# Attention with top-1 experts on one core: SyncE's transfers in the program's order, the row maxima split on VectorE, one block's sums inverted in place

## The chip, the cores and the metric

The kernel runs on one core of a Trainium2 chip. The metric is device time in microseconds of one launch, the median of several executions. A profile is one further execution; its own time is given beside its span below.

## The reference

The input `x` has 4 batches of 2048 tokens of 512 numbers. Each token is normalised, and `xn` goes through two branches that are added to `x`: an attention with 16 heads of 32 numbers, and a top-1 mixture of experts in which 8 experts take at most 100 tokens each, over all batches.

```python
x = L0_attn_x
xn = _layernorm(x)
x = x + _L0_attn_ref(xn, ...) + _L0_ffn_ref(xn, ...)

# attention
q, k, v = heads(xn @ w_qkv)
q, k = spectral_filter(q, mask), spectral_filter(k, mask)   # a linear map on each head's 32 numbers
attn = softmax(q @ k.T / sqrt(32))                          # 2048 x 2048 for each head
out = (attn @ v) @ w_out + b_out

# experts
probs = softmax(hs @ w_gate); best = argmax(probs)
location = cumsum(one_hot(best)) - 1                        # kept where location < 100
out = gate * (dispatched @ w_expert + b_expert)             # zero for the others
```

## The kernel before

**Groups, blocks, windows.** The 16 heads are worked four at a time, so there are 16 groups `k` (4 batches x 4 head groups; `k % 4` is the head group, and every fourth group ends a batch). A group has four blocks `n` of 512 queries. A block walks over 16 tiles `j` of 128 keys, two tiles to a window: 8 windows to a block, 32 to a group (`GW`), 512 in all. Here window w of a group is counted from that group's start; windows 24 to 31 belong to its block 3.

**One tile `j`.** For two pairs of heads `u`, TensorE first writes minus the row maxima into two banks of the array of 8 PSUM banks (`shift`, with `negm` as operand), then the scores of a later block, whose maxima are being taken (`max_matmuls`, two more banks), then this block's own scores on top of the shift (`scores`). ScalarE takes the exponentials into the tiles `even` and `odd`; VectorE reduces the later block's scores to maxima (`max_reduce`, tile `part`). Then come the products with `v` of the tile before (`products`, one bank), which VectorE adds to `num`. The banks are handed out in rotation by `bank()` and `turns`.

**The row maxima** run 40 steps of the stream ahead of the exponentials, so that a block's maxima are complete in window 5 of the block before it. `max_negate` (L469) makes `neg`; `max_close` (L474) runs in the next window: TensorE transposes `neg` into a bank (`pn`), ScalarE copies it to `rest`, GpSimd splits it into three bf16 parts that add up to it (`row`: three casts, two subtractions), and three DMAs of 4 KB spread them into `negm`, which the first `shift` of the next block reads.

**The sum of the exponentials** is built in the tile `even` by GpSimd (`add_to`, two adds to a window) and by an accumulating DMA from `odd` (`pair`, 1 MB to a window, GpSimd's queue).

**A block's end** (`close_steps`, L627) is spread over the windows of the next block, counted from its first: window 2 `fold` (row sums by TensorE, copied to `den`, written to DRAM), 3 `fetch` (read back as 128x16, `few`), 4 `invert` (a reciprocal on VectorE, written to DRAM), 5 `spread` (four broadcast reads to `factor`), 7 `divide` (`ot` on GpSimd), 8 and 9 the output projection into `y`, 10 an accumulating DMA of `y` to the output. The very last block uses `close_last`.

**The stage of the next batch.** In a group with `k % 4 == 2` the tokens of the next batch are loaded in four chunks of 1 MB (tag `xs`, two buffers), measured by VectorE (`measure`), given the output bias by GpSimd and written to the output (`first_sums`). At that group's end the first two chunks are loaded again, and in the next group they are normalised by ScalarE and transposed.

**What sets the order.** TensorE, VectorE, ScalarE and GpSimd are called through `InOrder` (L71): their instructions stay in the order in which the program makes them. Steps are entered in an agenda, a list for every window (`at`, L747); the first half of a window's list runs after its even tile, the rest after its odd one. SyncE's DMAs are made by plain `nc.sync` calls: the planner of the language may bring them forward, wherever it reckons that they can run. SyncE works through its own queue in order, and an entry that waits for data or for a buffer holds up those behind it. All wrapped instructions carry line L82 in the profile, SyncE's DMAs their own.

Of the kernel before, what the change touches and what calls it, by code (L numbers as in the profile page):

```python
# [12 lines left out]
F32 = mybir.dt.float32  # L13
# [88 lines left out]
def attention_and_top1_experts(ctx: ExitStack, tc: tile.TileContext, a: dict, out: bass.AP):  # L102
# [14 lines left out]
    def bank():  # L117

        return array[:, next(turns), :]
# [69 lines left out]


    on = SimpleNamespace(tensor=nc.tensor, vector=nc.vector, scalar=nc.scalar, gpsimd=nc.gpsimd)
    def filter_weights(c):
        for s in range(2):
            pt, pw = bank(), bank()
            for r in range(NR):
                on.tensor.transpose(
                    pt[:, r * P : (r + 1) * P], raw[s, r // 2][:, r % 2, c * P : (c + 1) * P], ident
                )
            if s == 0:
                both = probs(c == 1)  # L200
            wt = both[:, s]
            on.scalar.copy(wt[:, 0, :], pt)
            for r in range(NR):
                at = slice(r * P, (r + 1) * P)
                on.tensor.matmul(pw[:, at], lhsT=wt[:, 0, at], rhs=filt, start=True, stop=True)
            on.scalar.copy(wt[:, 1, :], pw)
            nc.sync.dma_start(out=wd[c][:, :, s, :], in_=wt[:, 1, :].rearrange("p (r n) -> p r n", r=NR))

    xnT = seq.tile([P, NR, S], F32, name="xnT")

# [1 line left out]
    def token_stage(b):  # L212
# [5 lines left out]

        def load(n, name="xs"):
            held[n] = chunk(name)  # L220
            nc.sync.dma_start(out=held[n], in_=x[b, n])

        def measure(i):
            on.vector.bn_stats(stats[:, i, :], held[i // TQ][:, i % TQ, :])
# [5 lines left out]

        def first_sums(n):

            nc.sync.dma_start(out=o[b, n], in_=held[n])

        def scale(first=0, last=NT):
            at = slice(first, last)
# [142 lines left out]

    def load_qkv_weights(k):  # L380
        wg[k] = weights.tile([P, NR, 3, P], F32, name="wg", bufs=1)
        nc.sync.dma_start(out=wg[k], in_=wd[k % NG])

    def load_out_weights(k):
        c = k % NG
        wo[k] = weights.tile([P, DM], F32, name="wo")
        nc.sync.dma_start(out=wo[k], in_=a["L0_attn_w_out"][c * P : (c + 1) * P, :])

    def columns(out, lhsT, rhs, **flags):

# [82 lines left out]

    def max_close(k, n):  # L474

        pn = bank()[0 : HG * TQ, 0:P]
        on.tensor.matmul(pn, lhsT=negs.pop((k, n)), rhs=ident, start=True, stop=True)
        rest = small.tile([HG * TQ, P], F32, name="rest")
        row = small.tile([HG * TQ, 3, P], BF16, name="row", bufs=2)
        on.scalar.copy(rest, pn)  # L480
        on.gpsimd.tensor_copy(row[:, 0, :], rest)
        for i in (1, 2):
            on.gpsimd.tensor_tensor(rest, rest, row[:, i - 1, :], ALU.subtract)
            on.gpsimd.tensor_copy(row[:, i, :], rest)
        negms[k, n] = qkv.tile([P, QB], BF16, tag="negm", name="negm", bufs=3)
        for i in range(3):
            nc.sync.dma_start(out=negms[k, n][i::DH, :], in_=row[:, i, :])


    taken = {}  # L490
# [1 line left out]
    def expert_steps():  # L492


        def begin():
            w_exp = chunk("w_exp")
            nc.sync.dma_start(out=w_exp, in_=a["L0_ffn_w_expert"].rearrange("(r p) n -> p r n", p=P))
            b_exp = work.tile([P, DM], F32, tag="b_exp", name="b_exp", bufs=1)
            nc.sync.dma_start(out=b_exp, in_=a["L0_ffn_b_expert"].partition_broadcast(P))
            entries = small.tile([P, NTAB, ST, 2], F32, name="entries")  # L500
            for i, table in enumerate(tables):
                nc.sync.dma_start(out=entries[:, i], in_=table.rearrange("(t p) c -> p t c", p=P))
# [12 lines left out]
            bound = {"bounds_check": B * S - 1, "oob_is_err": False}  # L515
            taken.update(mv=mv, w_exp=w_exp, b_exp=b_exp, entry=entry, index=index, bound=bound, xg=xg)
# [110 lines left out]
    def close_steps(k, n, num, acc):  # L627

        b = k // NG
        held = {}  # L630

        def fold():
            den = work.tile([P, QB], F32, tag="den", name="den", bufs=1)
            on.scalar.copy(den, row_sums([acc]))
            held["sums"] = scratch.tile([HG, QB], F32, name="sums")
            nc.sync.dma_start(out=held["sums"], in_=den[0::DH, :])


        def fetch():
            held["few"] = small.tile([P, HG * QB // P], F32, name="few", bufs=2)  # L640
            nc.sync.dma_start(out=held["few"], in_=held["sums"].rearrange("h (c e) -> (h c) e", e=HG * QB // P))

        def invert():
            on.vector.reciprocal(held["few"], held["few"])
            held["inverse"] = scratch.tile([HG, QB], F32, name="inverse")
            nc.sync.dma_start(
                out=held["inverse"].rearrange("h (c e) -> (h c) e", e=HG * QB // P), in_=held["few"]
            )

        def spread():  # L650
            held["factor"] = work.tile([P, QB], F32, tag="factor", name="factor", bufs=1)
            for h in range(HG):
                nc.sync.dma_start(
                    out=held["factor"][DH * h : DH * (h + 1)], in_=held["inverse"][h].partition_broadcast(DH)
                )

        def divide():
            held["ot"] = work.tile([P, QB], F32, tag="ot", name="ot", bufs=1)
            on.gpsimd.tensor_tensor(held["ot"], num, held["factor"], ALU.mult)

        def result(t):
            if t == 0:
                held["y"] = chunk("y")
            on.scalar.copy(held["y"][:, t, :], project(k, held["ot"], t))

        def add():
            on.gpsimd.dma_start(out=o[b, n], in_=held["y"], accum_op=ALU.add)

        steps = [(2, fold), (3, fetch), (4, invert), (5, spread), (7, divide)]
        return steps + [(8, result, 0), (8, result, 1), (9, result, 2), (9, result, 3), (10, add)]  # L670

    def close_last(k, n, num, tiles, y):
# [9 lines left out]
        for t in range(TQ):  # L682
            on.vector.tensor_tensor(y[:, t, :], y[:, t, :], project(k, ot, t), ALU.add)
            if t % 2 == 1:
                nc.sync.dma_start(out=o[b, n, :, t - 1 : t + 1, :], in_=y[:, t - 1 : t + 1, :])


    load, measure, scale, normalize, turn, first_route, first_bias, first_sums = token_stage(0)
# [22 lines left out]
    nc.gpsimd.memset(nobody, 0.0)  # L711
    nc.gpsimd.memset(nobody[:, :, 0], float(FAR))
    for table in tables:
        nc.sync.dma_start(out=table.rearrange("(t p) c -> p t c", p=P), in_=nobody)

    load_out_weights(0)
    first_projections = projections(0)
    for step in first_projections[:2]:
        step()
    ahead, first_projections = first_projections[2:7], first_projections[7:]  # L720
    on.tensor, on.vector, on.scalar, on.gpsimd = (
        InOrder(tc, engine) for engine in (nc.tensor, nc.vector, nc.scalar, nc.gpsimd)
    )
    closing = {}
    for i, item in enumerate(stream[:MAX_AHEAD]):
# [21 lines left out]
    def at(window, step, *args):  # L747
        agenda[window].append(lambda: step(*args))
# [30 lines left out]
    def plan(k):  # L779
# [16 lines left out]
            return  # L796
        at(start + GW // 2, load_out_weights, k + 1)
        if k + 2 < B * NG:
            at(start + GW - 1, load_qkv_weights, k + 2)
        if k == 0:  # L800
            at(len(first_projections), load_qkv_weights, 1)
        first, last = len(first_projections) + 2 if k == 0 else 0, GW - 1
        if c == NG - 2 and b + 1 < B:

            at(start + 10, begin_stage, b + 1)
            for n in range(NQ):
                at(start + 11 + 4 * n, in_stage, 0, n)
                at(start + 18 + 4 * n, in_stage, 7, n)
            for i in range(NT):
                at(start + 13 + i, in_stage, 1, i)  # L810
                at(start + 14 + i, in_stage, 6, i)
            at(start + GW - 2, in_stage, 2)
            at(start + GW - 2, in_stage, 0, 0)
            at(start + GW - 1, in_stage, 0, 1)
        elif c == NG - 1:

            for n in (2, 3):
# [23 lines left out]
    for k in range(B * NG):  # L841
        plan(k)
        for n in range(NQ):
            num = work.tile([P, QB], F32, tag="num", name="num")
            tiles = {}
            for w in range(NW):
# [7 lines left out]
                for j in (even, odd):  # L854
# [14 lines left out]
                    while full_blocks:  # L869
                        block = full_blocks.pop(0)  # L870
                        max_negate(*block)
                        at(window + 1, max_close, *block)
                    if left:
                        products(*left)
                    left = k, n, j, tiles[j], num
# [6 lines left out]
                        adds[window + 2] = tiles[even], tiles[even - WIN]  # L882
                if last and w == NW - 2:
                    y = chunk("xs")
                    nc.sync.dma_start(out=y, in_=o[B - 1, n])
# [44 lines left out]
```

## Time and profile before

| | |
|---|---|
| median of 3 runs | 4603.65 us (4592.69 to 4610.5) |
| the profiled execution, its own time | 4607.95 us |
| its span | 4606.1 us |
| TensorE, matmuls | 4435.0 us busy, 96% of the span |
| VectorE | 3102.1 us, 67% |
| GpSimd | 3001.0 us, 65% |
| ScalarE | 2596.2 us, 56% |
| DMAs issued by GpSimd (queue q0) | 606.88 MB, 66.6% of 16 engines |
| DMAs issued by SyncE (queue q1) | 91.56 MB, 6.4% of 16 engines |

PE is TensorE, PEld its weight loads, DVE VectorE, ACT ScalarE, POOL GpSimd, SP SyncE. Matmuls overlap, and the ends of busy times are modelled, so a busy TensorE is not one at its peak. The granted clock is TensorE's, as a share of full speed. An idle time in brackets behind an instruction names what ended it.

### The profile page before, as it was taken

The page shows a single profiled execution, that of the slowest core. Times are in us where ns is not written, and L with a number is a line of the kernel's source. Part 1 is how long each engine was busy: PE and PEld are TensorE (multiplying, and loading weights), DVE is VectorE, ACT ScalarE, POOL GpSimd, SP SyncE. Part 2 cuts the span into 40 slices and gives each one's busy share as a digit, 9 for nine tenths or more (in the row PEclk, how much of TensorE's full clock was granted, in tenths as well). Part 3 has the DMA queues.
Part 4 walks back from the last instruction along what each step waited for, and adds up shares of the span by engine and source line. Part 5 has one row for each costly group of instructions (what it writes and reads, how often), then busy time and mean ns, then how long its engine had stood idle before and what let it go on. Part 6 is the DMA issues. An engine that isn't in the chain of part 4 may idle for free.

```text
span 4606.1 us, 106228 instructions
## 1 busy us (share of the span) xinstructions
PE 4435.0 (96%) x44438; PEld 1886.8 (41%) x44438; DVE 3102.1 (67%) x3625; ACT 2596.2 (56%) x4945; POOL 3001.0 (65%) x2081
## 2 busy tenths in 40 slices
PE   6999999989999999998999999999999999999986
PEld 3444443433434344443444434343343434434431
DVE  4666776765676767775567766776567676777772
ACT  3445555555555555556455555555555565555654
POOL 0467766765676666775577666767567675777766
PEclk9999999989999999999999999999999999999998
DMA  5567777886776877787577776878767776787876
GB/s 117 137 153 149 152 157 149 186 184 137 142 151 140 163 147 159 151 205 177 120 145 154 158 154 134 165 163 191 158 125 150 155 152 127 151 169 163 162 159 143
DMA packets 193234, 708.90 MB, mean 154 GB/s; under 512 B 47778, under 2 KB 54084, under 8 KB 127344
## 3 DMA queue, kind: packets, MB, share of 16 engines
q0 software_dynamic: 110576, 606.88, 66.6%
q1 hardware_dynamic: 77800, 91.56, 6.4%
q8 instruction: 348, 5.70, 0.5%
q10 hardware_dynamic: 4376, 3.67, 0.4%
q14 instruction: 134, 1.10, 0.1%
HBM read 77.09 MB, written 89.99 MB: 36 GB/s over the span
## 4 chain that ended last, share of the span: by engine, by line
PE 85%; DMA 7%; POOL 3%; issue 3%; ACT 1%; DVE 1%; SPq 0%; ACTq 0%; POOLq 0%; DVEq 0%
PE array L82 85%; DMA even<-odd 2%; POOL even L82 2%; DMA few<-sums 1%; DMA sums<-den 1%; DMA negm<-row 1%; DVE part L82 1%; ACT odd L82 1%; DMA wg<-wd 0%; POOL ot L82 0%; DMA wd<-in_L_attn_w_qkv_dram 0%; POOL table L82 0%; ACT even L82 0%; PE array L393 0%; POOL rest L82 0%
## 5 line engine op out<-in xcount | busy, mean ns | idle before, releaser
L82 DVE TENSOR_REDUCE part<-array 128x2 f32<-128x1024 f32 (+1 forms) x2312 | 2433.6, 1097 | 1271.2 <-PE array L82 1259.4
L82 POOL TENSOR_TENSOR even<-even 128x1024 f32<-128x1024 f32 x892 | 2179.2, 2568 | 218.9 <-DMA even<-odd 217.0
L82 PE MATMUL array<-k,q 32*128 32x512 f32 x8192 | 2233.1, 623 | 8.5 <-issue 4.7
L82 PE MATMUL array<-q,k 32*128 32x512 f32 x8192 | 2059.8, 596 | 1.4 <-issue 1.4
L82 ACT ACTIVATE even<-array 128x512 f32<-128x512 f32 x2048 | 1065.4, 601 | 506.0 <-PE array L82 484.6
L82 ACT ACTIVATE odd<-array 128x512 f32<-128x512 f32 x2048 | 1060.7, 602 | 451.7 <-issue 237.7
L82 POOL DMA_DIRECT2D even<-odd x511 | 463.9, 908 | 1149.1 <-ACT odd L82 929.7
L82 PEld LDWEIGHTS array<-k,q 32*128 32x128 f32 x8192 | 812.1, 184 | 196.8 <-issue 76.1
L82 PE MATMUL array<-negm,ones_b 3*128 3x512 bf16 x4096 | 800.9, 383 | 55.7 <-DMA negm<-row 29.4
L82 PEld LDWEIGHTS array<-q,k 32*128 32x128 f32 x8192 | 752.1, 186 | 13.9 <-issue 5.1
L82 DVE TENSOR_TENSOR num<-num,array 128x512 f32<-128x512 f32 x960 | 651.1, 678 | 63.0 <-PE array L82 46.5
L82 PEld LDWEIGHTS <-ones_b 3*128 3x128 bf16 x4096 | 204.0, 92 | 926.8 <-issue 781.6
L82 PE MATMUL array<-even,v 128*32 128x512 f32 x4096 | 549.5, 609 | 9.8 <-ACT odd L82 9.7
L82 PE MATMUL array<-odd,v 128*32 128x512 f32 x4096 | 550.4, 608 | 3.3 <-ACT even L82 3.1
L82 PE MATMUL array<-xnT,wg 128*32 128x512 f32 x4032 | 461.6, 592 | 2.2 <-DMA wg<-wd 1.2
L82 PE MATMUL array<-wo,ot 128*32 128x512 f32 x2048 | 258.7, 596 | 19.6 <-POOL ot L82 19.5
L82 PEld LDWEIGHTS array<-xnT,wg 128*32 128x32 f32 x4032 | 131.8, 110 | 304.5 <-issue 268.8
L82 PEld LDWEIGHTS array<-even,v 128*32 128x32 f32 x4096 | 80.9, 108 | 400.8 <-ACT odd L82 388.2
L82 PEld LDWEIGHTS array<-odd,v 128*32 128x32 f32 x4096 | 81.3, 108 | 399.2 <-ACT even L82 388.5
L82 PEld LDWEIGHTS array<-wg,xnT 128*32 128x32 f32 x8192 | 226.1, 110 | 38.1 <-issue 22.6
L82 ACT COPY y<-array 128x512 f32<-128x512 f32 x252 | 147.5, 586 | 163.4 <-PE array L82 163.2
L82 PE MATMUL array<-wg,xnT 128*32 128x128 f32 x8192 | 237.0, 273 | 0.5
(140 smaller groups left out, 1436.0 us busy)
## 6 DMA issues: line engine op xcount, KB each, us to landing
even<-odd POOLq DMA_DIRECT2D x511, 1024.0 KB
out_dram<-y POOLq DMA_DIRECT2D x63, 1024.0 KB
xs<-in_L_attn_x_dram SPq DMA_DIRECT2D x31, 1024.0 KB
out_dram<-xs SPq DMA_DIRECT2D x16, 1024.0 KB
factor<-inverse SPq DMA_DIRECT2D x252, 64.0 KB
wg<-wd SPq DMA_DIRECT2D x16, 768.0 KB
wo<-in_L_attn_w_out_dram SPq DMA_DIRECT2D x16, 256.0 KB
negm<-row SPq DMA_DIRECT2D x192, 4.0 KB
```

What stands on the lines that cost most here:

```text
L82: done = act(*args, **kwargs)
```

## The change

1. SyncE gets the `InOrder` wrapper too, from the point where the other engines have it: all its DMAs keep the program's order.
2. Some steps move in the agenda. The load of a group's projection weights (`wg`) is entered for window 30, not 31. In the stage, the loads of the four chunks stand at windows 11, 15, 20, 24 (before: 11, 15, 19, 23) and the writes `first_sums` at 19, 23, 28, 32 (before: 18, 22, 26, 30); bias and measurement of chunks 2 and 3 come one window later; the second load of chunk 0 stays at 30, that of chunk 1 moves from 31 to 33, `scale` from 30 to 31.
3. `max_close` does its split on VectorE, three casts from PSUM and two subtractions in PSUM, in four slots of the bank of `pn`. ScalarE's copy and GpSimd's five instructions go. The step is put at the head of its window's list, not at its end.
4. The last block but one, (15, 2), is closed by `fold_here`: a reciprocal on VectorE of all 128x512 sums straight out of PSUM, with no way through DRAM, and its later steps come four windows sooner: `divide` at 3, projections at 4 and 5, the accumulating DMA at 6.

```diff
     def max_close(k, n):
-        pn = bank()[0 : HG * TQ, 0:P]
-        on.tensor.matmul(pn, lhsT=negs.pop((k, n)), rhs=ident, start=True, stop=True)
-        rest = small.tile([HG * TQ, P], F32, name="rest")
+        pn = bank()[0 : HG * TQ, :].rearrange("p (i n) -> p i n", n=P)
+        on.tensor.matmul(pn[:, 0], lhsT=negs.pop((k, n)), rhs=ident, start=True, stop=True)
         row = small.tile([HG * TQ, 3, P], BF16, name="row", bufs=2)
-        on.scalar.copy(rest, pn)
-        on.gpsimd.tensor_copy(row[:, 0, :], rest)
-        for i in (1, 2):
-            on.gpsimd.tensor_tensor(rest, rest, row[:, i - 1, :], ALU.subtract)
-            on.gpsimd.tensor_copy(row[:, i, :], rest)
+        for i in range(3):
+            if i > 0:
+                on.vector.tensor_tensor(pn[:, i], pn[:, i - 1], row[:, i - 1, :], ALU.subtract)
+            on.vector.tensor_copy(row[:, i, :], pn[:, i])
         negms[k, n] = qkv.tile([P, QB], BF16, tag="negm", name="negm", bufs=3)
         for i in range(3):
-            nc.sync.dma_start(out=negms[k, n][i::DH, :], in_=row[:, i, :])
+            on.sync.dma_start(out=negms[k, n][i::DH, :], in_=row[:, i, :])
...
+        def fold_here():
+            held["factor"] = work.tile([P, QB], F32, tag="factor", name="factor", bufs=1)
+            on.vector.reciprocal(held["factor"], row_sums([acc]))
...
+        if (k, n) == (B * NG - 1, NQ - 2):
+            return [(2, fold_here), (3, divide), (4, result, 0), (4, result, 1), (5, result, 2), (5, result, 3), (6, add)]
...
-    on.tensor, on.vector, on.scalar, on.gpsimd = (
-        InOrder(tc, engine) for engine in (nc.tensor, nc.vector, nc.scalar, nc.gpsimd)
+    on.tensor, on.vector, on.scalar, on.gpsimd, on.sync = (
+        InOrder(tc, engine) for engine in (nc.tensor, nc.vector, nc.scalar, nc.gpsimd, nc.sync)
     )
...
         if k + 2 < B * NG:
-            at(start + GW - 1, load_qkv_weights, k + 2)
+            at(start + GW - 2, load_qkv_weights, k + 2)
...
             at(start + 10, begin_stage, b + 1)
-            for n in range(NQ):
-                at(start + 11 + 4 * n, in_stage, 0, n)
-                at(start + 18 + 4 * n, in_stage, 7, n)
+            for n, (come, go) in enumerate(((11, 19), (15, 23), (20, 28), (24, GW))):
+                at(start + come, in_stage, 0, n)
+                at(start + go, in_stage, 7, n)
             for i in range(NT):
-                at(start + 13 + i, in_stage, 1, i)
-                at(start + 14 + i, in_stage, 6, i)
-            at(start + GW - 2, in_stage, 2)
+                at(start + 13 + i + i // 8, in_stage, 1, i)
+                at(start + 14 + i + i // 8, in_stage, 6, i)
+            at(start + GW - 1, in_stage, 2)
             at(start + GW - 2, in_stage, 0, 0)
-            at(start + GW - 1, in_stage, 0, 1)
+            at(start + GW + 1, in_stage, 0, 1)
...
                         max_negate(*block)
-                        at(window + 1, max_close, *block)
+                        agenda[window + 1].insert(0, lambda block=block: max_close(*block))
```

All other `nc.sync.dma_start` calls become `on.sync.dma_start` (the first loads, made before the wrapper is set, stay free). One of them is the load of the output rows that the very last block adds to (L885, entered in window 510); others are the expert stage's `w_exp`, `b_exp` and `entries` (L497 to L502, entered in window 18 of group 12, with two reductions of `entries` on VectorE in the same step).

More of the change, by code (lines that the diff above doesn't have):

```diff
@@ L191, in attention_and_top1_experts @@
     on = SimpleNamespace(tensor=nc.tensor, vector=nc.vector, scalar=nc.scalar, gpsimd=nc.gpsimd)
+    on.sync = nc.sync
     def filter_weights(c):
@@ L206, in filter_weights @@
             on.scalar.copy(wt[:, 1, :], pw)
-            nc.sync.dma_start(out=wd[c][:, :, s, :], in_=wt[:, 1, :].rearrange("p (r n) -> p r n", r=NR))
+            on.sync.dma_start(out=wd[c][:, :, s, :], in_=wt[:, 1, :].rearrange("p (r n) -> p r n", r=NR))
     xnT = seq.tile([P, NR, S], F32, name="xnT")
@@ L220, in load @@
             held[n] = chunk(name)
-            nc.sync.dma_start(out=held[n], in_=x[b, n])
+            on.sync.dma_start(out=held[n], in_=x[b, n])
         def measure(i):
@@ L231, in first_sums @@
         def first_sums(n):
-            nc.sync.dma_start(out=o[b, n], in_=held[n])
+            on.sync.dma_start(out=o[b, n], in_=held[n])
         def scale(first=0, last=NT):
@@ L381, in load_qkv_weights @@
         wg[k] = weights.tile([P, NR, 3, P], F32, name="wg", bufs=1)
-        nc.sync.dma_start(out=wg[k], in_=wd[k % NG])
+        on.sync.dma_start(out=wg[k], in_=wd[k % NG])
     def load_out_weights(k):
@@ L386, in load_out_weights @@
         wo[k] = weights.tile([P, DM], F32, name="wo")
-        nc.sync.dma_start(out=wo[k], in_=a["L0_attn_w_out"][c * P : (c + 1) * P, :])
+        on.sync.dma_start(out=wo[k], in_=a["L0_attn_w_out"][c * P : (c + 1) * P, :])
     def columns(out, lhsT, rhs, **flags):
@@ L496, in begin @@
             w_exp = chunk("w_exp")
-            nc.sync.dma_start(out=w_exp, in_=a["L0_ffn_w_expert"].rearrange("(r p) n -> p r n", p=P))
+            on.sync.dma_start(out=w_exp, in_=a["L0_ffn_w_expert"].rearrange("(r p) n -> p r n", p=P))
             b_exp = work.tile([P, DM], F32, tag="b_exp", name="b_exp", bufs=1)
-            nc.sync.dma_start(out=b_exp, in_=a["L0_ffn_b_expert"].partition_broadcast(P))
+            on.sync.dma_start(out=b_exp, in_=a["L0_ffn_b_expert"].partition_broadcast(P))
             entries = small.tile([P, NTAB, ST, 2], F32, name="entries")
             for i, table in enumerate(tables):
-                nc.sync.dma_start(out=entries[:, i], in_=table.rearrange("(t p) c -> p t c", p=P))
+                on.sync.dma_start(out=entries[:, i], in_=table.rearrange("(t p) c -> p t c", p=P))
             entry = small.tile([P, ST, 2], F32, name="entry1")
@@ L635, in fold @@
             held["sums"] = scratch.tile([HG, QB], F32, name="sums")
-            nc.sync.dma_start(out=held["sums"], in_=den[0::DH, :])
+            on.sync.dma_start(out=held["sums"], in_=den[0::DH, :])
+        def fold_here():
+            held["factor"] = work.tile([P, QB], F32, tag="factor", name="factor", bufs=1)
+            on.vector.reciprocal(held["factor"], row_sums([acc]))
         def fetch():
             held["few"] = small.tile([P, HG * QB // P], F32, name="few", bufs=2)
-            nc.sync.dma_start(out=held["few"], in_=held["sums"].rearrange("h (c e) -> (h c) e", e=HG * QB // P))
+            on.sync.dma_start(out=held["few"], in_=held["sums"].rearrange("h (c e) -> (h c) e", e=HG * QB // P))
         def invert():
@@ L645, in invert @@
             held["inverse"] = scratch.tile([HG, QB], F32, name="inverse")
-            nc.sync.dma_start(
+            on.sync.dma_start(
                 out=held["inverse"].rearrange("h (c e) -> (h c) e", e=HG * QB // P), in_=held["few"]
@@ L652, in spread @@
             for h in range(HG):
-                nc.sync.dma_start(
+                on.sync.dma_start(
                     out=held["factor"][DH * h : DH * (h + 1)], in_=held["inverse"][h].partition_broadcast(DH)
@@ L684, in close_last @@
             if t % 2 == 1:
-                nc.sync.dma_start(out=o[b, n, :, t - 1 : t + 1, :], in_=y[:, t - 1 : t + 1, :])
+                on.sync.dma_start(out=o[b, n, :, t - 1 : t + 1, :], in_=y[:, t - 1 : t + 1, :])
     load, measure, scale, normalize, turn, first_route, first_bias, first_sums = token_stage(0)
@@ L713, in attention_and_top1_experts @@
     for table in tables:
-        nc.sync.dma_start(out=table.rearrange("(t p) c -> p t c", p=P), in_=nobody)
+        on.sync.dma_start(out=table.rearrange("(t p) c -> p t c", p=P), in_=nobody)
     load_out_weights(0)
@@ L884, in attention_and_top1_experts @@
                     y = chunk("xs")
-                    nc.sync.dma_start(out=y, in_=o[B - 1, n])
+                    on.sync.dma_start(out=y, in_=o[B - 1, n])
                 window += 1
```

## The prediction

> **What bounds it now.** I read the page's busy times and chain first, then TensorE's waits, then the chain and SyncE's queue around one of the waits, then the granted clock, then a quiet window.
>
> ```profile
> PE 4435.0 (96%) x44438; PEld 1886.8 (41%) x44438; DVE 3102.1 (67%) x3625; ACT 2596.2 (56%) x4945; POOL 3001.0 (65%) x2081
> PE 85%; DMA 7%; POOL 3%; issue 3%; ACT 1%; DVE 1%; SPq 0%; ACTq 0%; POOLq 0%; DVEq 0%
> PE array L82 <- DMA negm<-row: 29.4, 5, 8.8
> PE array L82 <- POOL ot L82: 19.5, 10, 7.7
> SPq L885 <- DMA out_dram<-y: 32.4, 1, 32.4
> ```
>
> TensorE sets the time; it is idle for 171 us, in few, long waits, and the last line is one entry of SyncE's queue that held it for 32 us. SyncE's queue and the chain, at the end of group 2 (the stage):
>
> ```profile
> 917.67 0.38 SPq L221 DMA_DIRECT2D xs<-in_L_attn_x_dram  x1
> 921.66 0.53 SPq L636 DMA_DIRECT2D sums<-den  x1
> 957.04 0.38 SPq L221 DMA_DIRECT2D xs<-in_L_attn_x_dram  x1
> 958.41 2.21 SPq L487 DMA_DIRECT2D negm<-row  x3
> ...
> 921.66 11.71 DMA sums<-den
> 933.39 8.54 DMA few<-sums
> 960.09 11.15 DMA negm<-row
> 942.02 0.25 DVE L82 RECIPROCAL few<-few 128x16 f32<-128x16 f32 x1 [6.64 <-DMA few<-sums]
> 943.40 0.58 PE L82 MATMUL array<-negm,ones_b 3*128 3x512 bf16 x1 [2.47 <-DVE part L82]
> 943.00:949.60 6.60, 6.20 (x31) 2.40 (x34) 4.80 (x7) 2.17 (x4) 6.60 (x5) 0.50 0.81 169
> ```
>
> Small transfers stand behind 1 MB loads that the planner brought forward (the load at 917.67 belongs to window 30 and ran in window 26): 8 KB took 11.71 us, 4 KB 11.15 us. In quiet blocks `sums` takes about 6 us. VectorE waits for `few` with its reductions behind it, TensorE for VectorE's banks; after 2.47 us of idleness the granted clock (the column before the last two) is 0.50 for 6.6 us. A window later `negm` is late, two more later the next `few`.
>
> **The gain at the stages.** TensorE's idle times there are 2.47 + 1.64 + 7.07 + 6.44 = 17.6 us after group 2, 1.60 + 8.75 + 6.53 = 16.9 after group 6, 1.60 + 6.81 + 6.01 = 14.4 after group 10. The half-clock stretches last 23.8, 20.4 and 20.4 us; the parts in which TensorE works (15.5, 10.0, 13.7) cost half of themselves, 7.7 + 5.0 + 6.9. Sum: 68.5 us. In the written order `fold` and `fetch` of blocks 2 and 3 have no 1 MB transfer just ahead of them, and `negm` goes ahead of `wg` and `xs` in window 30. What is late next: SyncE runs ahead of the windows, so chunk 0's load follows `sums` at window 11 and `first_sums` follows it at 19, both ahead of a `fetch` whose reciprocal comes some 10 us later; and chunk 0 of the second pass, behind `wg` (1.75 MB) from window 30, is normalised in 32, 13 us later. A 1 MB load moves at full pace only between the `pair` transfers (5 us of each 6.2 us window), so these are close. I take back 2 us a stage, 0 and 12 at the ends. Gain 62.
>
> **Queues that the moved steps pass.** In SyncE's queue the load of chunk 2 (window 20) waits for the write of chunk 0 to land, with block 1's `inverse` and `factor` behind it; GpSimd needs `factor` three windows later, some 20 us on, so that costs nothing unless a 1 MB transfer takes over 15 us. The second load of chunk 1 (33) waits for the write of chunk 3 (32), with block 3's `sums` behind it; `few` is due two windows later. `wg` in window 30 waits for the last projection, made by window 29: nothing. `max_close` at the head of its list puts its transpose up to half a window earlier in TensorE's queue, at the same length, and its three DMAs (0.53 us of SyncE each) ahead of that window's loads.
>
> **Group 15.** The load of L885, brought forward to group 15's first half, blocks `sums`: TensorE idles 12.54 us from 4423.8 and then runs 5.2 us at half clock: 15 us, which go, as the load now stands behind window 6 of block 2. The `negm` wait at 4510 (5.40 us) goes with GpSimd's casts, but `ot` is next in GpSimd's queue and only 2 us sooner: gain 2.
>
> **The tail.**
>
> ```profile
> 4578.21 3.47 PE L82 MATMUL array<-wo,ot 128*32 128x512 f32 x16 [7.65 <-POOL ot L82]
> 4593.17 1.32 POOL L82 DMA_DIRECT2D out_dram<-y  x1 [3.99 <-ACT y L82]
> ```
>
> Today block (15, 2) leaves its projections and its accumulating DMA (10 us, SyncE waits 10.3 us for it at the end) behind everything else. Early, its inversion costs VectorE about 3.2 us (a 128x128 reciprocal took 0.91; it grows with the columns), hidden, since no maxima are left (without that cover up to 3 us, the adds to `num` being behind it), and its DMA then stretches the last `pair` (the same neighbour stretched one to 15.80 us at 4537). The end is then the last output write, some 4 us after its issue at about 4591 to 4594, not 4604.8: gain 8, between 0 and 15.
>
> **Smaller gains.** Seven waits for `ot` at the turn of a group (1.2 to 1.9 us, 9 in all) follow GpSimd's five split instructions (3 x 0.28 + 2 x 0.42 and gaps, 2 us): gain 7. A `negm` wait behind `entries` at 3575 (1.35) and one for `wg` (1.22): 2.5.
>
> **The price of the split.** The quiet window in which a close falls:
>
> ```profile
> 1667.95 0.68 DVE L82 TENSOR_TENSOR num<-num,array 128x512 f32<-128x512 f32 x1
> 1669.08 2.42 DVE L82 TENSOR_REDUCE part<-array 128x1 f32<-128x512 f32 x3 [0.45 <-PE array L82]
> 1667.60 0.38 PE L82 MATMUL array<-square,neg 128*16 128x128 f32 x2
> 1669.00 0.59 PE L82 MATMUL array<-k,q 32*128 32x512 f32 x2
> L82 DVE COPY logits<-array 128x32 f32<-128x32 f32 x16 | 2.9, 184 | 0.0
> L82 DVE TENSOR_TENSOR chosen<-array,gate 128x128 f32<-128x128 f32 x4 | 1.2, 292 | 0.4
> ```
>
> VectorE's 67% hides that here both engines are full: a tile asks VectorE for 2 x 1.22 + 0.68 = 3.12 us and TensorE for 3.14. No cast of 16x128 from PSUM is in the trace. A copy of 32 columns takes 184 ns[...]; a subtraction 292. Each depends on the one before, which adds 35 ns (gap between `stats` and `mv`): 3 x 0.284 + 2 x 0.292 + 4 x 0.035 = 1.58 us. [...]the bank of `pn` stays shut for all of it, where ScalarE's copy freed it after 0.25.
>
> Who waits: the next eight banks are two shifts and two maxima for each `u`, and the eighth, the second maxima bank of `u` = 0, is the bank of `pn`. TensorE gets there at 1669.00, 1.0 us after the transpose's end at 1667.98. VectorE is free at 1668.63 (its add), done at 1668.63 + 1.58 = 1670.21: TensorE stalls 1.2 us, and 0.9 where VectorE is not behind (after a projection). It can't win this back, being the bound. From 0.5 (short instructions, VectorE ahead) to 1.6 (all of it), I take 1.0, between the two cases. With 63 closes whose next maxima are running: 63 us, ends 32 and 100. [...]here 1.97 us at 1456 was enough and 2.10 us at 263 was not. [...] No stall under 1.7 us stands alone before a halving here, so I count none.
>
> **Another price.** Group 12, window 18: `w_exp`, `b_exp` and `entries` are issued only after window 14's `negm`, not 100 to 400 us ahead, and VectorE's two reductions of `entries` wait with all maxima behind them. `entries` are 8-byte packets, 3584 of them; beside `pair` one set took about 7 us (3576.6 to 3584). From 3632 they have 30 us and need about that: 3 us, between 0 and 16.
>
> **Sum.** 4607.95 - 62 - 17 - 8 - 7 - 2.5 + 63 + 3 = 4577.5 us for the profiled execution; it lies 4.3 us above the median of the runs, so 4573 for a median.
>
> **Rivals.** (a) *The split is cheaper*: VectorE catches up in time, 0.5 us a close. For it: in block 2 of group 2, eight `bn_stats` pairs (0.87 us each) lengthened the block by only 2 us (67.5 against 65.6 in group 5, from first exponential to first exponential). Against it: those shut no bank. 63 becomes 32: 4542. (b) *The stage waits stay*: loads at windows 11, 19 and 30 make `few`, the measurements or ScalarE's normalising late, 8 to 10 us a stage with the half clock. For it: every one of these margins is under 5 us, and a load issued at 917.67 was still on the wire at 933. Against it: `pair` leaves gaps. 24 us back: 4597. (c) *Slower*: the split's full length and a second stall behind it, because VectorE's lag meets the next tile's add bank (0.3 us short in my count): 2.0 us a close, 126 us: 4636. It turns the gain of 96.5 into a loss from 93.5 / 63 = 1.5 us a close, and into 0.5% from 1.85. (d) That the order doesn't change is ruled out by the loads seen ahead of their windows.
>
> **Chances.** My forecast 0.5, (a) 0.22, (b) 0.16, (c) 0.12. About 0.5%, 23 us, is what a measurement of this kernel can tell from no change: below 4580.6 or above 4626.7. The forecast's own range is 4557 to 4590; 0.33 of its 0.5 lies below 4580.6. Faster: 0.33 + 0.22 (a) + 0.02 (b) = 0.57; same: 0.17 + 0.13 (b) = 0.30; slower: (c) and 0.01 of (b), 0.13. Range: the lower end takes in most of (a), whose shortest ends (tail 15, stages 68) reach 4530; the upper takes in (b): 4532 to 4620.
>
> **What would show it.** Right: no wait of TensorE for `negm`; `few` waits under 2 us at stage ends; stretches 880 to 1080 and its like without half clock; block (15, 1) 15 us shorter; window 6 of a quiet block about 1 us longer (6.8 to 7.8) with TensorE waiting for VectorE's `row`. Wrong: window 6 unchanged (then a), ScalarE waiting for `xs`, or VectorE for `few` or `stats`, in stages (b), window 7 longer too (c).

## The result, and the profile after

The changed kernel takes 4583.6 us (median of 5 runs, 4580.68 to 4584.95) where the kernel before takes 4603.65 beside it: a ratio of 0.9956, 95% interval 0.994 to 0.9973. It is faster by 20 us, or 0.44%, which is real but under the half per cent that the prediction took as its bound: by that bound it is "same", to which it had given 0.30, and not "faster", to which it had given 0.57. The forecast was 4573, its range 4532 to 4620. The profiled execution took 4580.68 us, its span 4578.9.

Busy times and chain of the changed kernel, from its page:

```profile
PE 4473.4 (98%) x44438; PEld 1884.3 (41%) x44438; DVE 3188.4 (70%) x3943; ACT 2587.4 (57%) x4880; POOL 2897.2 (63%) x1761
PE 89%; DMA 4%; DVE 4%; issue 2%; ACT 1%; POOL 1%; DVEq 0%; SPq 0%; ACTq 0%; POOLq 0%
```

In the chain DMAs fell from 7% to 4% and GpSimd from 3% to 1%; VectorE rose from 1% to 4%. Waits for transfers went, waits for VectorE came. Waits of the changed kernel (engine, what it waited for: us in all, times, longest):

```profile
PEld array L82 <- DVE row L82: 58.4, 60, 1.1
...
PE array L82 <- POOL ot L82: 8.3, 5, 4.4
...
PE array L82 <- DMA negm<-row: 3.9, 2, 2.9
PE array L82 <- DVE row L82: 3.1, 13, 0.3
```

TensorE's waits for `negm` fell from 29.4 to 3.9 us, those for `ot` from 19.5 to 8.3. The new line is the first: 60 times the loading of weights waits about 1 us for `row`, VectorE's split. (The wait stands with PEld: what waits is a weight load of the next maxima, as at 1663.23 below.)

SyncE's queue of the changed kernel at the end of group 2 (start, us, entry), the stretch that the prediction showed:

```profile
900.31 0.40 SPq L82 DMA_DIRECT2D xs<-in_L_attn_x_dram  x1
932.76 0.54 SPq L82 DMA_DIRECT2D sums<-den  x1
938.36 0.34 SPq L82 DMA_DIRECT2D few<-sums  x1
...
959.88 2.48 SPq L82 DMA_DIRECT2D negm<-row  x3
962.41 0.49 SPq L82 DMA_DIRECT2D wg<-wd  x1
962.96 0.42 SPq L82 DMA_DIRECT2D xs<-in_L_attn_x_dram  x1
```

The last 1 MB load ahead of `sums` was issued 32 us earlier, and `few` follows `sums` after 5.6 us instead of 11.7. `negm` goes ahead of `wg` and `xs`. Stretches of 200 us around the ends of groups 2, 6 and 10 of the changed kernel (window, length, then busy us of PE, PEld, DVE, ACT and POOL; the column before the last two is the granted clock):

```profile
880.00:1080.00 200.00, 196.40 (x1798) 81.98 (x1790) 144.41 (x185) 131.79 (x244) 131.64 (x79) 1.00 0.86 192
1980.00:2180.00 200.00, 195.26 (x1843) 82.89 (x1840) 146.42 (x187) 131.09 (x243) 135.19 (x82) 1.00 0.88 196
3100.00:3300.00 200.00, 193.46 (x1741) 81.02 (x1736) 143.10 (x181) 130.14 (x240) 131.56 (x79) 0.99 0.86 191
```

The same stretch of group 2 in the kernel before:

```profile
880.00:1080.00 200.00, 181.17 (x1606) 77.65 (x1606) 129.59 (x156) 123.02 (x230) 130.08 (x91) 0.94 0.84 190
```

TensorE is busy 196.4 us instead of 181.2, at full clock instead of 0.94. The quiet window with a close (window 14 of group 5), in the changed kernel, first TensorE's transpose of the maxima:

```profile
1660.69 0.38 PE L82 MATMUL array<-square,neg 128*16 128x128 f32 x2
```

VectorE:

```profile
1661.04 0.68 DVE L82 TENSOR_TENSOR num<-num,array 128x512 f32<-128x512 f32 x1
1661.63 0.27 DVE L82 CAST row<-array 16x128 bf16<-16x128 f32 x1
1661.94 0.29 DVE L82 TENSOR_TENSOR array<-array,row 16x128 f32<-16x128 f32 x1
...
1662.90 0.28 DVE L82 CAST row<-array 16x128 bf16<-16x128 f32 x1
1663.11 2.51 DVE L82 TENSOR_REDUCE part<-array 128x1 f32<-128x512 f32 x3
```

TensorE's weight loads in the same window:

```profile
1661.77 0.50 PEld L82 LDWEIGHTS array<-k,q 32*128 32x128 f32 x2
1663.23 0.18 PEld L82 LDWEIGHTS array<-k,q 32*128 32x128 f32 x1 [0.95 <-DVE row L82]
```

The transpose ends at 1661.07 (1660.69 + 0.38); VectorE is at its add until the first cast starts at 1661.63, splits until 1663.18, and TensorE goes on at 1663.23. The window lasts 7.82 us, where the kernel before needs 6.73.

Where the 27.2 us of the span went, measured in windows from first exponential to first exponential:

| part | forecast | measured |
|---|---|---|
| split: window 6 of all 64 blocks | +63 | +60.2 |
| stages: the two blocks at the end of groups 2, 6, 10 (without their windows 6) | -62 | -22.5, -18.6, -13.7, together -54.8 |
| group 15 (without windows 6) | -17 | -20.6 |
| tail, behind the last exponential | -8 | -7.1 (36.7 to 29.6) |
| smaller: first windows of groups 1, 4, 6, 8, 12 and 14 (-8.4), window 7 of blocks (0, 0) and (12, 0) (-2.5) | -9.5 | -10.9 |
| `entries` in group 12, window 18 | +3 | 0 (its block grew by 0.9, the split) |
| all else, the start included | 0 | +6.0 |
| sum, profiled execution | -30.5 | -27.2 |

### The profile page after: what moved, and what is told of

Same layout as the page of the kernel before. It is cut to its first block, busy times and chain, and to the rows that moved or that the text cites. A ratio compares the mean times of both kernels' runs of the same rounds, so it can differ in the third digit from the quotient of the medians.

```text
span 4578.9 us, 106335 instructions
## 1 busy us (share of the span) xinstructions
PE 4473.4 (98%) x44438; PEld 1884.3 (41%) x44438; DVE 3188.4 (70%) x3943; ACT 2587.4 (57%) x4880; POOL 2897.2 (63%) x1761
## 4 chain that ended last, share of the span: by engine, by line
PE 89%; DMA 4%; DVE 4%; issue 2%; ACT 1%; POOL 1%; DVEq 0%; SPq 0%; ACTq 0%; POOLq 0%
PE array L82 88%; DMA even<-odd 2%; DVE part L82 1%; DVE row L82 1%; DVE array L82 1%; ACT odd L82 0%; DVE num L82 0%; POOL even L82 0%; DMA inverse<-few 0%; DMA factor<-inverse 0%; DMA sums<-den 0%; DMA negm<-row 0%; PE array L394 0%; DMA wd<-in_L_attn_w_qkv_dram 0%; ACT xs L82 0%
## 5 line engine op out<-in xcount | busy, mean ns | idle before, releaser
L82 PE MATMUL array<-k,q 32*128 32x512 f32 x8192 | 2283.2, 621 | 12.9 <-issue 3.3
L82 PEld LDWEIGHTS array<-k,q 32*128 32x128 f32 x8192 | 824.3, 183 | 231.2 <-DVE num L82 66.2
L82 PEld LDWEIGHTS array<-q,k 32*128 32x128 f32 x8192 | 738.7, 185 | 14.6 <-issue 6.7
L82 PE MATMUL array<-even,v 128*32 128x512 f32 x4096 | 549.8, 608 | 10.6 <-ACT odd L82 9.7
```

What stands on the lines that cost most here:

```text
L82: done = act(*args, **kwargs)
```

## The experiments

Times are medians. Ratios are to the kernel before on the same chip, with 95% intervals. Not all kernels ran on one chip, so they are compared with each other by ratio.

**One part alone: the split.** The kernel before with VectorE's split at the head of the list.

```diff
-        on.scalar.copy(rest, pn)
-        on.gpsimd.tensor_copy(row[:, 0, :], rest)
...
+            on.vector.tensor_copy(row[:, i, :], pn[:, i])
...
-                        at(window + 1, max_close, *block)
+                        agenda[window + 1].insert(0, lambda block=block: max_close(*block))
```

> The kernel before with the split on VectorE, at the head of its list, and nothing else of the change. Theory: 63 closes at 1.08 us, less GpSimd's waits (some 7 us at group turns, 5 us for negm at the end): 4603.65 + 68 - 12 = 4660 us. Rival, the split helps at the stages because negm is ready sooner there: 4600 to 4630.

Measured 4669.02 us, ratio 1.0137 (1.012 to 1.0154): 65 us slower, window 6 longer by 1.06 us in the mean of its blocks. The split costs what the trace of before said.

**One part undone: the split.** The changed kernel with ScalarE's copy and GpSimd's five instructions put back.

```diff
...
-            on.vector.tensor_copy(row[:, i, :], pn[:, i])
...
+        on.scalar.copy(rest, pn)
+        on.gpsimd.tensor_copy(row[:, 0, :], rest)
...
```

> The changed kernel with the split of the maxima given back to ScalarE's copy and GpSimd's five instructions (still at the head of its window's list). Theory: the split on VectorE costs TensorE about 1.08 us in each of 63 closes (68 us), and saves GpSimd's waits (about 7 us for ot at group turns, 2 us at the end): 4583.6 - 68 + 9 = 4525 us, window 6 of a quiet block back from 7.85 to 6.8 us. Rival, the split is nearly free and the lost microseconds come from elsewhere: 4580 to 4600, window 6 unchanged.

Measured 4549.48 us, ratio 0.9886 (0.987 to 0.9903): faster than the changed kernel by 32 us by the ratios, not 58. Window 6 gives back 65 us, but about 33 are lost elsewhere. Blocks (3, 0), (7, 0) and (11, 0) grow by 6.7, 7.6 and 2.8 us, (15, 1) and (15, 2) by 8.1 and 4.8, and the first window of five groups by about 1.5 each. SyncE's queue there, with the old split:

```profile
950.29 0.43 SPq L82 DMA_DIRECT2D wg<-wd  x1
950.78 0.42 SPq L82 DMA_DIRECT2D xs<-in_L_attn_x_dram  x1
```

ScalarE, two windows later:

```profile
969.64 1.52 ACT L82 ACTIVATE xs<-xs,shift,rstd 128x512 f32<-128x512 f32 x2 [4.89 <-DMA xs<-in_L_attn_x_dram]
971.07 1.06 ACT L82 ACTIVATE even<-array 128x512 f32<-128x512 f32 x2
```

`wg` (0.75 MB), moved to window 30, goes just ahead of the second load of chunk 0, which takes 18.7 us; ScalarE needs it after 14, waits 4.89 us, and the exponentials stand behind it (5.21 and 5.14 us at the other two stages). This is what rival (b) described. In the changed kernel ScalarE needs it 17 us after its issue and does not wait. Two things give it the 3 us more. TensorE's stall in window 6 is about 1 of them. The rest is the issue: `wg` stands behind `negm`, and goes out 5.7 to 6.3 us into window 30 in the changed kernel, but only 8.0 to 8.7 with GpSimd's split. The third try below has a stall of 0.7 us with GpSimd's split, and ScalarE waits 3.9 to 5.3 us there. In block (15, 1) VectorE waits 5.89 us for `few`; why it comes late there is open.

**One part alone: the order.** The kernel before with SyncE's wrapper and nothing else; windows, split and tail are the old ones.

```diff
-    on.tensor, on.vector, on.scalar, on.gpsimd = (
-        InOrder(tc, engine) for engine in (nc.tensor, nc.vector, nc.scalar, nc.gpsimd)
+    on.tensor, on.vector, on.scalar, on.gpsimd, on.sync = (
+        InOrder(tc, engine) for engine in (nc.tensor, nc.vector, nc.scalar, nc.gpsimd, nc.sync)
...
```

> The kernel before with SyncE's DMAs in the program's order and nothing else: the windows of the loads and writes as before, the split as before. If the order alone does it: the waits for few at the stage ends and in group 15 go, 62 + 15 us: 4525 to 4530. If the moved windows are needed: the block at group 15 is 15 us shorter, but TensorE still waits for negm or few at the ends of groups 2, 6 and 10, since negm stands behind the loads of windows 30 and 31: 4570 to 4590.

Measured 4548.12 us, ratio 0.9873 (0.9857 to 0.989): the order alone is worth 56 us and beats the whole change. The six stage blocks lose 57 us and (15, 1) loses 14, without any moved window. The tail grows from 36.7 to 41.5 us.

**The order undone.** The changed kernel without SyncE's wrapper.

```diff
-    on.tensor, on.vector, on.scalar, on.gpsimd, on.sync = (
-        InOrder(tc, engine) for engine in (nc.tensor, nc.vector, nc.scalar, nc.gpsimd, nc.sync)
+    on.tensor, on.vector, on.scalar, on.gpsimd = (
+        InOrder(tc, engine) for engine in (nc.tensor, nc.vector, nc.scalar, nc.gpsimd)
```

> The changed kernel with SyncE's transfers in the planner's order again, and the new windows kept. Theory (the written order ends the waits of the stages, the new windows do little): waits for `few` and `negm` return, each pair of blocks at a stage is some 17 us longer and block (15, 1) 14 us longer: 4583.6 + 3 x 17 + 14 = about 4649. Rival (the new windows alone end them): 4583 to 4595.

Measured 4643.06 us, ratio 1.0079 (1.0062 to 1.0096), some 57 us above the changed kernel. Its queue of SyncE at the end of group 2:

```profile
938.08 0.38 SPq L222 DMA_DIRECT2D xs<-in_L_attn_x_dram  x1
938.56 1.25 SPq L635 DMA_DIRECT2D sums<-den  x1
953.11 0.33 SPq L645 DMA_DIRECT2D few<-sums  x1
```

A 1 MB load stands half a microsecond ahead of `sums` again, and `sums` takes 14.5 us. Block (2, 3) is 13.1 us longer than in the changed kernel, (15, 1) 14.4. The moved windows do nothing against this without the order. They do help the blocks behind it: (3, 0), (7, 0) and (11, 0) are 7.1 to 8.3 us shorter than in the kernel before, where with the split alone they are 0.2 us shorter to 0.5 longer.

**The inversion undone.** The changed kernel with block (15, 2) closed like all others.

```diff
-        if (k, n) == (B * NG - 1, NQ - 2):
-            return [(2, fold_here), (3, divide), (4, result, 0), (4, result, 1), (5, result, 2), (5, result, 3), (6, add)]
```

> The changed kernel with block (15, 2) inverted like all others (through memory, in the windows behind its end) instead of at once. Theory (the early inversion shortens the tail): the stretch behind the last exponential is 7 us longer again, the blocks before it stay: 4591. Rival (SyncE's order had already shortened the tail): no difference, 4583.

Measured 4602.68 us, ratio 0.9989 (0.9979 to 0.9999): the inversion is worth 0.33%, 15 us, more than either theory said. The tail is 38.9 us instead of 29.6, and the last block 2.5 us longer, together 11.8; the rest of the 15 is within the intervals.

**Why the split costs 1 us: length.** The changed kernel with the five instructions done twice, the first time with no use.

```diff
-        for i in range(3):
...
+        for again in range(2):
+            for i in range(3):
...
```

> The changed kernel with the five instructions of the split done twice over in the same bank (the first time over with no use). Theory (TensorE waits for VectorE's whole length): each close costs a further 1.58 us, 63 of them 100 us: about 4684, window 6 at 9.4 us. Rival (part of the length lies beside other work, and only part of a longer one does): 60 us, 4644.

Measured 4748.83 us, ratio 1.0296 (1.0279 to 1.0314): 156 us above the changed kernel's ratio, more than both. Weight loads of TensorE in two such windows (PEld idles through the whole wait of 2.42 us; the matmuls already issued fill part of it):

```profile
1734.49 0.18 PEld L82 LDWEIGHTS array<-k,q 32*128 32x128 f32 x1 [2.42 <-DVE row L82]
...
1804.48 0.18 PEld L82 LDWEIGHTS array<-k,q 32*128 32x128 f32 x1 [2.42 <-DVE row L82]
```

The stretches behind these waits, by windows:

```profile
1732.80:1739.40 6.60, 5.01 (x31) 1.76 (x34) 4.66 (x11) 1.50 (x3) 1.95 (x3) 0.74 0.60 141
...
1802.80:1807.80 5.00, 3.41 (x31) 1.46 (x34) 4.49 (x10) 1.49 (x3) 1.26 (x3) 1.00 0.50 107
```

The two waits are alike, with 1.59 us in which TensorE has nothing to do (from the matmuls' modelled ends). After the first the clock halves (0.74 granted over 6.60 us, which is about 3.4 us at half), after the second it doesn't (1.00). Against the changed kernel window 6 grows by 1.47 us in 25 blocks, by 2.8 to 3.4 in 22 and by 4.3 to 4.5 in 15. So the wait itself costs 1.47, which is all of the time by which the bank is held longer (3.58 us instead of 2.11), and in 37 of 62 closes half clock comes on top, for 1.3 to 3.0 us more.

**Why: the shut bank or VectorE's time, first try.** The changed kernel with a copy to SBUF, so that the bank is free after 0.29 us, and VectorE splitting from SBUF.

```diff
...
+        on.scalar.copy(rest, pn)
+        on.vector.tensor_copy(row[:, 0, :], rest)
+        for i in (1, 2):
+            on.vector.tensor_tensor(rest, rest, row[:, i - 1, :], ALU.subtract)
+            on.vector.tensor_copy(row[:, i, :], rest)
```

> The changed kernel with ScalarE's copy of the transposed maxima to SBUF put back, and the five instructions of the split still on VectorE, but from SBUF. It takes the bank out of the wait and leaves VectorE's work. Theory of the shut bank: TensorE no longer stalls at the second maxima bank, window 6 goes from 7.85 to 6.8 to 7.1 us, and the time to 4520 to 4535. Rival, VectorE is full and its 1.5 us a close are passed on to TensorE whatever the bank: window 6 stays at 7.6 to 7.9, time 4570 to 4585.

Measured 4746.36 us, ratio 1.0308 (1.0291 to 1.0325): neither. VectorE in this kernel:

```profile
1709.42 2.34 DVE L82 TENSOR_TENSOR rest<-rest,row 16x128 f32<-16x128 f32 x1
1711.79 0.38 DVE L82 CAST row<-rest 16x128 bf16<-16x128 f32 x1
1712.21 6.23 DVE L82 TENSOR_TENSOR rest<-rest,row 16x128 f32<-16x128 f32 x1
```

GpSimd at the same time:

```profile
1706.96 4.66 POOL L82 TENSOR_TENSOR even<-even 128x1024 f32<-128x1024 f32 x2 [1.53 <-DMA even<-odd]
...
1712.14 4.93 POOL L82 TENSOR_TENSOR even<-even 128x1024 f32<-128x1024 f32 x2
1716.73 1.55 POOL L82 TENSOR_TENSOR ot<-num,factor 128x512 f32<-128x512 f32 x1
```

A subtraction of 16x128 takes 0.28 us in its undisturbed form and 6.23 beside three GpSimd instructions in a row. 51 of 192 casts and 19 of 128 subtractions took over 1 us. The casts and subtractions of the changed kernel, which read PSUM, never took more than 0.29. So in these runs it is the instructions out of SBUF that were stretched, and not those out of PSUM; by what, the traces do not show. This test of the bank is thus spoilt, but for seven closes (in blocks (k, 0)) in which the five instructions took together under 1.3 us: their window 6 is 0.00 to 0.11 us longer than before, and window 7 in five of them 0.5 to 0.7.

**Second try.** The changed kernel with a rotation that passes over the bank of `pn` once (`turns` leaves out a bank in `kept` the next time).

```diff
...
+        kept.append(next(turns))
+        pn = array[0 : HG * TQ, kept[-1], :].rearrange("p (i n) -> p i n", n=P)
```

> The changed kernel, whose rotation of PSUM banks passes over the bank of `pn` once: TensorE's next maxima (the eighth bank after `pn`) go to the bank behind it, and `pn`'s bank comes back eight banks later. VectorE's five instructions stay as they are. Theory (TensorE waits for the shut bank): the wait in window 6 goes, VectorE's 1.58 us are made up later by its free time, window 6 falls by 0.6 to 1.0 us again, and the time by 40 to 63 us: 4521 to 4545. Rival (TensorE pays for VectorE's time, by whichever bank): the wait moves to the next bank that VectorE hands back, window 6 stays 0.9 us longer than before, and the time stays at 4575 to 4590.

Measured 4590.72 us, ratio 0.9964 (0.9952 to 0.9977), window 6 as in the changed kernel. That looks like the rival, but the line shows another wait. TensorE's weight loads in this kernel:

```profile
1667.63 0.18 PEld L82 LDWEIGHTS array<-k,q 32*128 32x128 f32 x1 [0.71 <-ACT odd L82]
```

The bank that takes the turn holds the scores of the same tile's first pair of heads, which ScalarE is still reading. All eight banks are in use: there is none to pass on to. This run does not tell the theories apart.

**Third try.** The kernel with the old split, in which ScalarE makes its copy six times over: the bank is held without any work for VectorE.

```diff
...
+        for again in range(6):
+            on.scalar.copy(rest, pn)
...
```

> The changed kernel with the old split (ScalarE copies the maxima out of `pn`, GpSimd splits them), in which ScalarE makes the copy six times, five of them with no use: the bank of `pn` is held for some 1.4 us, and VectorE has no work for it. Theory (a shut bank costs TensorE by itself): TensorE waits for `rest` 0.5 to 0.9 us in window 6, which goes from 6.8 to 7.3 or 7.7 us; 62 closes make 31 to 56 us over the same kernel with one copy (4549): 4580 to 4605. Rival (VectorE's time is what costs): window 6 stays within 0.2 us of 6.8, 4549 to 4562. If ScalarE's exponentials come late instead, TensorE waits for `even` or `odd` and not for `rest`.

Measured 4575.09 us, ratio 0.9928 (0.9901 to 0.9956), 0.42% above the kernel with one copy; window 6 grows by 0.68 us in the mean, 44 us in all. (The profiled spans differ by 33.5 us, the ratios by only 19: less than the theory's 31, since the profile of the kernel with one copy was the fastest of its runs, and some 10 us were won outside the windows 6.) TensorE's transpose in the quiet window of this kernel:

```profile
1656.78 0.38 PE L82 MATMUL array<-square,neg 128*16 128x128 f32 x2
```

ScalarE:

```profile
1657.19 1.69 ACT L82 COPY rest<-array 16x128 f32<-16x128 f32 x6
```

And TensorE's weight loads behind it:

```profile
1658.94 0.18 PEld L82 LDWEIGHTS array<-k,q 32*128 32x128 f32 x1 [0.57 <-ACT rest L82]
```

This shows the cause: VectorE has no work here, and TensorE waits for the bank all the same. Held from the end of the transpose to the last reader, in a quiet block, against what window 6 loses:

| kernel | bank held | price in window 6 |
|---|---|---|
| before: one copy | 0.29 us | 0 |
| six copies on ScalarE | 1.72 | 0.70 |
| the change | 2.11 | 1.08 |
| split twice (clock whole) | 3.58 | 2.55 |

The price is the time that the bank is held less 1.03 us, whoever holds it. What VectorE's time costs by itself stays open beyond the seven closes above.

**A better version.** The order and the inversion on the kernel before; old windows, old split.

> The kernel before with two parts of the change alone: SyncE's transfers in written order, and block (15, 2) inverted at once; windows, split and the place of `max_close` are the old ones. Theory (the two gains add up, and the old split costs less than the new): the order alone stood 55 us under the kernel before, the inversion is worth 12 to 18 us beside it: ratio 0.984, about 4533. Rival (the tail in written order has another end, and the inversion brings nothing): as with the order alone, 0.987, 4548.

Measured 4537.13 us, ratio 0.9856 (0.9827 to 0.9885): 46 us faster than the changed kernel, and the lowest ratio of all. By the ratios the inversion adds 8 us to the order alone, less than the 12 to 18 expected, and the two intervals lie over each other. Its tail is 27.6 us instead of 41.5 with the order alone, its last block 2.6 us longer.

The same with `max_close` at the head of its list:

> As the kernel with order and inversion, and `max_close` at the head of its window's list as in the changed kernel. Theory (the head brings `negm` ahead of the loads of windows 11 and 30): the waits behind these loads go, 3 to 10 us less than without it, about 4527. Rival (it also makes VectorE's banks or ScalarE's copy collide): the same or up to 5 us more.

Measured 4544.79 us, ratio 0.9864 (0.9836 to 0.9892). The intervals lie over each other: the head brings nothing that can be seen. This kernel and the changed one with the old split differ in the moved windows alone. The six stage blocks are 55.4 us shorter than in the kernel before here, and 41.4 there; ScalarE waits for `xs` at one stage (2.86 us) here, and at all three there. So with the old split the moved windows cost 14 us at the stages.

## Why the prediction was right

**The split's price** was 1.0 us a close, 63 us; measured 60.2, with a median of 1.08. The prediction's own steps hold: the casts took 278 ns and the subtractions 286 (from 284 and 292), the bank comes due 1.0 us after the transpose (1.03), VectorE is late by its add, and no clock is lost (1.00 granted in the quiet window). (The 284 ns of a cast were the author's estimate; the rows of the kernel before bear it out: 184 ns for a copy of 32 columns and 678 for an add of 512 make 1.03 ns a column, so 283 for 128.) That the bank of `pn` stays shut for the whole split was an assumption of the forecast; the mechanism, a shut bank in a full rotation, is shown by the bank held on ScalarE. The price is spread over 62 windows, not 63: behind the close in block (15, 2) no maxima are left, and its window 6 did not grow. VectorE's chain took 1.55 us (1661.63 to 1663.18), where the forecast had 1.58.

**The stages** were to give 62 and gave 54.8. Groups 2 and 6 came out at -22.5 and -18.6, where the measured idleness and half-clock cost, less 2 us each, said 23.3 and 19.9; group 10 gave only 13.7 of 19.3. There a wait of 2.92 us for `negm` at 3258 and 3.4 us at half clock (0.86 granted from 3250 to 3262) remain in window 7 of block (11, 0); the same window is 3.7 us shorter in the kernels with the inversion undone and with the bank passed over, so this one comes and goes. What the prediction did not separate is which half of the edit does it: the order alone, as two runs show. The moved windows, worth some 23 us in the blocks behind the stages without the order, add nothing to it, and cost 14 us with the old split.

**Group 15** gave 20.6 instead of 17: (15, 1) lost 16.6, the forecast 15 and a wait of 1.91 us for `ot` that the forecast had counted among its smaller gains. (15, 2) lost 5.5 instead of 2, of which the last block gave 2.0 back; there TensorE waits 4.36 us for `ot`, the wait that the prediction named as next.

**The tail** gave 7.1 of 8, but in part by luck. Without the inversion the tail of the changed kernel is 2.2 us longer than before (38.9 against 36.7), and with the order alone 4.8 us; the prediction had no such loss. The inversion takes 9.3 us off it. So 7.1 is a gain larger than forecast less a loss that was not foreseen. The inversion took 3.36 us (3.2 in the forecast), and the last `pair` transfer 12.9 us beside the early one of `y` (TensorE waits 5.25 us for it). VectorE's line in the changed kernel:

```profile
4519.76 3.36 DVE L82 RECIPROCAL factor<-array 128x512 f32<-128x512 f32 x1 [0.19 <-PE array L82]
```

TensorE's line behind that transfer:

```profile
4564.02 3.64 PE L82 MATMUL array<-even,ones 128*32 128x512 f32 x16 [5.25 <-DMA even<-odd]
```

**The smaller gains** gave 10.9 where 9.5 were forecast: 8.4 at the turn of six groups, 1.5 at the `negm` wait behind `entries`, 1.0 at the one for `wg`. Of the seven waits for `ot` that the forecast names, one is the 1.91 us in block (15, 1), counted above, and one is 0.39 us, not 1.2. `entries` cost nothing.

**The 10.6 us between forecast and median** are two things. The sum missed by 3.3 us, and part of that closeness is luck: the stages fell 7.2 us short, the tail 0.9, and 6.0 more came from places that nobody named, while the split, group 15, `entries` and the smaller gains came out 10.8 better than forecast. The other 7.2 are the step from a profiled execution to a median: it lay 4.3 us above its median before and 2.9 below it after.

**The rivals.** (a), 0.5 us a close, was rejected for the right reason: its witnesses shut no bank, and five of the seven closes with a free bank indeed cost about 0.6. (b) did not come about in this kernel, but does with the old split. That `pair` slows a 1 MB load holds: in the kernel before SyncE's queue moved 0.69 MB in 2 us while GpSimd's stood still (961 to 963), and 0.26 MB beside GpSimd's 0.26 (924 to 926). (c) did not come about; with twice the length, the half clock makes something worse of it, 3.7 us a close.

## What to carry to other kernels

Where banks go round in a full rotation, as here, the price of an engine's work in one of them is how long it is held beyond the moment at which its turn comes again (here 1.03 us after the transpose; the price was 0.70, 1.08 and 2.55 us for 1.72, 2.11 and 3.58 us held); read both moments in a quiet window before moving work into PSUM. A change whose sum comes out near the forecast can still be a poor whole, so run its parts alone: here the order and the inversion are worth 65 us, and the rest of the change takes 46 of them back. A transfer in written order is only as good as the place where it is written (behind `wg` and with the old split, chunk 0's load took 18.7 us and held ScalarE up for 4.89), so look at what stands just ahead of each small one.

## What the runs showed that was not expected

Small VectorE instructions whose operands are in SBUF took up to 6.7 us for 0.28 us of work, and the one of 6.23 us above ran beside three of GpSimd's instructions in a row and ended 0.16 us after the last. And no one length of idleness set off the half clock: in the kernel with the split done twice, gaps of 1.3 to 1.8 us in the same place of the same loop halved it in 37 of 62 closes and left it whole in 25. Of 39 gaps of 1.59 us, 21 halved it and 18 did not; the shortest that did was 1.54 us, the longest that did not 1.69. The forecast took 1.7 us as the shortest; in the kernel before, 0.72 was granted from 1456 to 1462, around an idleness of 1.97 us, and 1.00 behind one of 2.10 us at 263.
